# Neighbour choice kept as marks in the score tile, and turned into one-hots by TensorE and ScalarE

## The chip, the cores and the metric

The kernel runs on one core of one Trainium2 chip. The metric is the device time of one execution in microseconds (us); before the change the median of three runs is 13028.27 us, with 13025.54 and 13030.78 as the ends.

## The reference, cut to what matters

Two layers follow each other. Layer 0 cuts 16 images of 96 x 64 x 64 into windows of 8 x 8 pixels, finds for each of the 64 nodes of a window its nine nearest nodes, and takes the maximum of an edge function over them. Layer 1 is a state-space (Mamba) block, twice, over the 4096 pixels of each image, then a batch norm and a residual.

```python
nodes = win.reshape(Bw, C, WS * WS).transpose(0, 2, 1)      # Bw windows, 64 nodes, 96 channels
idx = knn_idx(nodes, K)                                      # K = 9 nearest by cosine distance, the node itself among them
x_j = jax.vmap(lambda n, i: n[i])(nodes, idx)
feat = jnp.concatenate([x_i, x_j - x_i], axis=-1)
h = jnp.einsum('bnkc,oc->bnko', feat, ew) + eb
h = jnp.max(gelu(h * es + et), axis=2)                       # over the nine neighbours
...
hstates = associative_scan(comb, (dA, dBx), axis=1)[1]       # layer 1, per image and layer
y = jnp.einsum('blds,bls->bld', hstates, Cm) + Dp * xc
```

## The kernel before

**Work and stages.** An image has eight rows of eight windows, 128 rows in all; a row has 512 pixels. Layer 0 works by rows, in two generators: `nearest` computes the scores of all node pairs and picks the eight nearest others, and `edges` gathers and evaluates them. Layer 1 works by items: 256 items, each one stretch of 512 pixels of one image in one of two layers, and an item has eight steps, one for each pair of states. These 2048 steps are the main loop.

**One step of the main loop.** `bcast` (L729, TensorE) spreads one row pair of the matrix B over the partitions into a PSUM tile `bt`, of which there is one buffer; `times_b` (L734, VectorE) multiplies it into `db` (PSUM, one buffer); the scan (L911, VectorE) runs over `da` and `db` into `hb`; GpSimd multiplies `hb` by C (L943); `folded` (L745, L747, TensorE) sums it into `y`. ScalarE makes `da` by three exponentials (L708), up to two steps ahead. `bt` of the next step is the first thing TensorE does in a step, `db` of the next step is made by VectorE after the scan, and `y` of the step before is folded last.

**What runs beside it.** The order on each engine is the order in which the program issues (`manual_schedule`). In each step the generators in `going` (an item's `norm`, `nearest`, `edges`, `tail`) are advanced by one `yield`, oldest first, and after them those in `preps` (`prelude`, the projections of the item after next). Products handed to `apart` are issued at the end of the step, and what uses them at the start of the next. From the ninth row on one row is started every 16 steps: `edges` of a row and `nearest` of the next one start in the same step, `nearest` ahead of `edges` in the list. Both have 16 stages of this kind, so a row takes 16 steps, and two items pass meanwhile. The first three rows run before the main loop (`drain`), and five rows after them run at twice the pace.

**The names used below.** The steps of one row's cycle are numbered 1 to 16. `edges` handles four of the eight windows in steps 1 to 8 and the other four in steps 9 to 16: three steps for the one-hot matrices `oh`, two for the products `pv` (L452, L453) and their copy `vu`, two for the gather products `t` (L468, L471) with their GELU (L476), one spare. In steps 8 and 16 `prelude` starts (`pj`, L608 and L620 with the Silu table), in steps 1 and 9 it goes on (`pj` L613, then the table of exp and ln again), in steps 2 and 10 come its product `pd` and the product `pow` of `tail` (L772), in steps 3 and 11 `pdta` (L646) with `e` and `rl` (L653, L654). In step 3 there are also `pf` of the next row's `nearest` (L340, its `y` at L343) and `pf2` of `edges` (L515). In step 4 `norm` issues `pc` (L581) with `sqv` (L583), and in step 5 `pvar` with `rs` (L588). In steps 6 and 14 the products with `dp_diag` (L742, L743) open a new `y`.

**PSUM.** `bt` takes one bank, `db` three, `y` two; all else shares the tag `mm` with two buffers. A new `mm` tile takes the buffer of the one before the last, and waits until that one has been read.

**The one-hots before.** VectorE's `max` gives the eight best scores of each node of a window pair, `max_index` their positions (L396, L909, in steps 12 to 15). The positions are written to DRAM (L401), read back onto 64 partitions by a broadcast DMA of 256 KB (L430), and compared with the partition's number: for one pair of windows by GpSimd (`is_equal`, L441), for the other by ScalarE (Abs L443, then Relu of 1 - x, L444).

Of the kernel before, what the change touches and what calls it, by code (L numbers as in the profile page):

```python
# [10 lines left out]
F32 = mybir.dt.float32  # L11
U16 = mybir.dt.uint16
BF16 = mybir.dt.bfloat16
AF = mybir.ActivationFunctionType
ALU = mybir.AluOpType
# [6 lines left out]
def tile_conv_knn_mamba(ctx: ExitStack, tc: tile.TileContext, w: dict, out: bass.AP):  # L22
# [8 lines left out]
    nc = tc.nc  # L31
# [4 lines left out]
    NN = WS * WS  # L36
    K = 9
    KO = K - 1
    NQ = H // WS
    NW = W // WS  # L40
    NP = NW // 2
    Q = 512
# [15 lines left out]
    const = ctx.enter_context(tc.tile_pool(name="const", bufs=1))  # L58
    dram1 = ctx.enter_context(tc.tile_pool(name="dram1", bufs=1, space=DRAM))
    dram = ctx.enter_context(tc.tile_pool(name="dram", bufs=3, space=DRAM))  # L60


    ident = const.tile([128, 128], F32, name="ident")
    make_identity(nc, ident)
    cmat = const.tile([C, C], F32, name="cmat")
    nc.vector.tensor_scalar(cmat, ident[:C, :C], -1.0 / C, None, ALU.add)
    node = const.tile([NN, 1], F32, name="node")
    nc.gpsimd.iota(node, pattern=[[0, 1]], base=0, channel_multiplier=1, allow_small_or_imprecise_dtypes=True)
    minus_node = const.tile([NN, 1], F32, name="minus_node")
    nc.vector.tensor_scalar(minus_node, node, -1.0, None, ALU.mult)  # L70
    neg1 = const.tile([128, 1], F32, name="neg1")
    nc.vector.memset(neg1, -1.0)
    eps_t = const.tile([128, 1], F32, name="eps_t")
# [4 lines left out]
    ohs = []  # L78
# [122 lines left out]
    pr = main.enter_context(tc.tile_pool(name="ring", bufs=2))  # L201
# [3 lines left out]
    pm = main.enter_context(tc.tile_pool(name="ps_m", bufs=2, space=PSUM))  # L205
# [102 lines left out]
    def half(h):  # L308
        return slice(h * CB, (h + 1) * CB)

    closing, opening, uses = [], [], []
# [17 lines left out]
    chosen_of = {}  # L329

    def nearest(b, q):

        nm = f"{b}_{q}"
        xr = pr.tile([C, Q], F32, tag="seq", name=f"x_{nm}", bufs=NSEQ)
        seqs[b, q] = xr
        nc.sync.dma_start(out=xr, in_=x[b].rearrange("c h w -> c (h w)")[:, bass.ts(q, Q)])
        yield
        yield
        pf = pm.tile([C, Q], F32, tag="mm", name=f"pf_{nm}")
        nc.tensor.matmul(pf, lhsT=fc1T, rhs=xr, start=True, stop=True)  # L340
        y = pr.tile([C, Q], F32, tag="y0", name=f"y_{nm}")
        nodes_of[b, q] = y
        nc.scalar.activation(  # L343
            y.rearrange("p (w r c) -> p r w c", w=NW, r=WS),
            pf.rearrange("p (r w c) -> p r w c", r=WS, w=NW),
            AF.Identity,
            bias=fc1_b[:, 0, :],
            scale=fc1_s[:, 0, :],
        )
        yield  # L350
        sq = pr.tile([C, Q], F32, tag="sq", name=f"sq_{nm}")
        nc.gpsimd.tensor_tensor(sq, y, y, ALU.mult)
        yield

        ss = pm.tile([C, Q], F32, tag="mm", name=f"ss_{nm}")
        nc.tensor.matmul(ss, lhsT=ones_cc, rhs=sq, start=True, stop=True)
        nc.scalar.copy(sq[0:1], ss[0:1])
        ss_d = dram.tile([1, Q], F32, tag="ss_d", name=f"ssd_{nm}")
        nc.sync.dma_start(out=ss_d, in_=sq[0:1])
        r4 = pr.tile([128, 2, QJ], F32, tag="r4", name=f"r4_{nm}")  # L360
        nc.sync.dma_start(out=r4[:, 1], in_=ss_d.rearrange("o (p j) -> (o p) j", j=QJ))
        yield
        yield

        nc.gpsimd.tensor_scalar(r4[:, 0], r4[:, 1], 1e-24, None, ALU.max)
        nc.gpsimd.tensor_tensor(r4[:, 0], r4[:, 0], mhalf, ALU.pow)
        nc.gpsimd.tensor_tensor(r4[:, 1], r4[:, 1], r4[:, 0], ALU.mult)
        nc.gpsimd.tensor_tensor(r4[:, 1], r4[:, 1], r4[:, 0], ALU.mult)
        yield
        r4_d = dram.tile([2, Q], F32, tag="r4_d", name=f"r4d_{nm}")  # L370
        nc.sync.dma_start(out=r4_d.rearrange("t (p j) -> p t j", j=QJ), in_=r4[:, 0:2])
        rn = pr.tile([C, Q], F32, tag="rs", name=f"rn_{nm}")
        nc.sync.dma_start(out=rn, in_=r4_d[0:1, :].to_broadcast([C, Q]))
        hs = hss[(b * NQ + q) % NHS]
        nc.sync.dma_start(out=hs[NN : NN + 1].rearrange("o w j -> o (w j)"), in_=r4_d[1:2, :])
        yield
        yield
        xn = pr.tile([C, Q], F32, tag="xn", name=f"xn_{nm}", bufs=1)
        nc.gpsimd.tensor_tensor(xn, y, rn, ALU.mult)
        yield  # L380


        sc = pm.tile([128, NP, NN], F32, tag="mm", name=f"sc_{nm}")
        hs4 = hs.rearrange("k (p h) j -> k p h j", h=2)
        for h in range(2):
            nc.tensor.matmul(sc[half(h)], lhsT=own, rhs=hs4[:, :, h, :], start=True, stop=False)
            for p in range(NP):
                nodes = xn[:, bass.ts(2 * p + h, NN)]
                nc.tensor.matmul(sc[half(h), p, :], lhsT=nodes, rhs=nodes, start=False, stop=(p == NP - 1))
        scs = pr.tile([128, NP, NN], F32, tag="scs", name=f"scs_{nm}", bufs=1)  # L390
        nc.scalar.copy(scs, sc)
        yield
        idx = pr.tile([128, NP, KO], U16, tag="idx", name=f"idx_{nm}")
        for p in range(NP):
            m1 = pr.tile([128, KO], F32, tag="m1", name=f"m1_{nm}_{p}")
            nc.vector.max(m1, scs[:, p, :])  # L396
            opening.append(partial(nc.vector.max_index, idx[:, p, :], m1, scs[:, p, :]))
            yield SLOT

        idx_d = dram.tile([NP, 128, KO], U16, tag="idx_d", name=f"idxd_{nm}")  # L400
        nc.sync.dma_start(out=idx_d.rearrange("p i k -> i p k"), in_=idx)  # L401
        chosen_of[b, q] = idx_d

    def taken():

# [10 lines left out]
    def edges(b, q):  # L416

        nm = f"{b}_{q}"
        y = nodes_of.pop((b, q))
        idx_d = chosen_of.pop((b, q))  # L420
        maxima = []

        def maximum(w):
# [2 lines left out]
                maxima.append(pr.tile([128, NP, NB3, NN], F32, tag="hq", name=f"hq_{nm}", bufs=1))  # L426
            return maxima[0][:, w]
        for hf in range(2):
            idb = pr.tile([NN, NP, NN * KO], U16, tag="idb", name=f"idb_{nm}_{hf}", bufs=1)
            nc.sync.dma_start(  # L430
                out=idb.rearrange("j w n -> j (w n)"),
                in_=idx_d.rearrange("(s p) i k -> s (p i k)", s=2)[hf : hf + 1].to_broadcast([NN, NP * NN * KO]),
            )
            yield


            for p in (1, 0):
                ohj = ohs[p][0:NN].rearrange("j w i k -> j w (i k)")
                numbers = idb[:, 2 * p : 2 * p + 2, :]
                if p == 0:  # L440
                    nc.gpsimd.tensor_scalar(ohj, numbers, node, None, ALU.is_equal)  # L441
                else:
                    nc.scalar.activation(ohj, numbers, AF.Abs, bias=minus_node)  # L443
                    nc.scalar.activation(ohj, ohj, AF.Relu, bias=1.0, scale=-1.0)  # L444
                yield
            vus = []
            for p in range(2):

# [11 lines left out]
            for p in range(2):  # L460
# [4 lines left out]
                for part in range(3):  # L465
# [9 lines left out]
                    j = part // 2  # L475
# [4 lines left out]
            if hf == 1:  # L480
# [8 lines left out]
                    bias=e_b[:, 0:1],  # L489
                    scale=e_s[:, 0:1],  # L490
# [3 lines left out]
                for h in range(2):  # L494
# [5 lines left out]
                    bias=e_b[:, 1:2],  # L500
                    scale=e_s[:, 1:2],
# [326 lines left out]

    FIRST = 3
    drain(nearest(0, 0))  # L830
    for q in range(FIRST):
        drain(nearest(0, q + 1), edges(0, q), *([prepared(q - 1)] if q else []))
    drain(nearest(0, FIRST + 1))

    AHEAD = 2
    order = [(n, p) for n in range(NI) for p in range(NPR)]
# [20 lines left out]
    bt = bcast(*order[0])  # L857
    db = times_b(*order[0], bt)
    going, preps = [several_at_once(edges(0, FIRST), 3)], []
    for _ in range(3):  # L860
        next(going[0])
# [3 lines left out]
    for r in range(FIRST + 1, NB * NQ):  # L865
        at = NPR * (r - FIRST) - 3 if r <= NQ else 16 * (r - NQ) + 29
        rows_at.setdefault(at, []).append((edges, r, 3 if r <= NQ else 1))
        if r > FIRST + 1:
            quick = r <= NQ + 1
            rows_at.setdefault(at - (9 if quick else 16), []).insert(0, (nearest, r, 2 if quick else 1))  # L870
    for m, (n, p) in enumerate(order):
        b, i, k = items[n]
        nm = f"{b}_{i}_{k}"
# [102 lines left out]
    with tc.tile_pool(name="bn", bufs=5) as pn:  # L976
        for b in range(NB):
            o = pn.tile([128, NJ, 1024], F32, tag="o", name=f"bo_{b}")
# [35 lines left out]
```

## Time and profile before

| | |
|---|---|
| median of three runs | 13028.27 us |
| the profiled execution | 13021.43 us |
| its span, first to last instruction | 13019.7 us |
| mean granted TensorE clock | 0.949 |
| VectorE busy | 11940.4 us (92%) |
| GpSimd busy | 11686.0 us (90%) |
| TensorE busy, matmuls | 11254.7 us (86%) |
| ScalarE busy | 10407.8 us (80%) |
| `oh` on GpSimd, L441 | 256 x 2855 ns |
| `oh` on ScalarE, L443 and L444 | 256 x 1134 ns and 256 x 1057 ns |
| first scan of the main loop | 263 us after the span's start |

The columns are times of one profiled execution on the one core. A line such as "L441 POOL TENSOR_SCALAR oh<-idb,node" is an instruction group by source line, engine and operation, with the tile it writes and those it reads. POOL is GpSimd, DVE VectorE, ACT ScalarE, PE TensorE, PEld its weight loads, SPq the queue on which the DMAs are issued. In a timeline a number in brackets is the idle time of that engine before the instruction, with what ended it.

### The profile page before, as it was taken

To read this page: it belongs to the slowest core of one execution; us is meant where nothing else is said; L and a number is where in the kernel's file an instruction comes from. 1 tells how busy PE (TensorE), PEld (TensorE's weight loads), DVE (VectorE), ACT (ScalarE), POOL (GpSimd) and SP (SyncE) were. 2 spreads that over 40 slices of the span, in tenths; PEclk is the share of its full clock that TensorE was granted. 3 is DMA by queue.
4 is the path that set the end of the run, shared out by engine and by line. 5 is a ranking of instruction groups with operands and counts; after the bars stand their busy time and mean duration, and the time that the engine had idled before them with its cause. 6 is when DMAs were issued, how large, how long until landed. Compare 5 with 4: busy or idle time off the path is not lost.

```text
span 13019.7 us, 155850 instructions
## 1 busy us (share of the span) xinstructions
PE 11254.7 (86%) x46920; PEld 4359.3 (33%) x46920; DVE 11940.4 (92%) x8270; ACT 10407.8 (80%) x16186; POOL 11686.0 (90%) x8644
## 2 busy tenths in 40 slices
PE   5889889888989989888888888988888888889872
PEld 2333333333333333333333333333333333333320
DVE  2699999999999999999999999999999999999995
ACT  4778888888888888888888888888888888888763
POOL 3699999999999999999999999999999999999993
PEclk8899999999999999999999999999999999999986
DMA  1233333333333333333333333333333333333336
GB/s 38 66 85 95 91 91 93 94 92 89 98 89 90 96 92 90 93 94 89 95 95 87 98 92 90 94 92 93 90 95 92 90 95 93 92 89 97 89 87 261
DMA packets 1031198, 1226.82 MB, mean 94 GB/s; under 512 B 429440, under 2 KB 560910, under 8 KB 1024208
## 3 DMA queue, kind: packets, MB, share of 16 engines
q1 hardware_dynamic: 1026352, 1191.59, 35.2%
q10 hardware_dynamic: 4000, 25.28, 0.5%
q8 instruction: 370, 6.06, 0.2%
q14 instruction: 476, 3.90, 0.1%
HBM read 706.83 MB, written 85.72 MB: 61 GB/s over the span
## 4 chain that ended last, share of the span: by engine, by line
POOL 27%; PE 19%; DVE 18%; ACT 13%; issue 9%; DMA 7%; SPq 6%; POOLq 0%; DVEq 0%; ACTq 0%
POOL hb L943 16%; DVE hb L911 11%; DVE db L734 6%; ACT da L708 5%; PE y L745 3%; SPq L690 2%; SPq L692 2%; DMA ct<-cd 2%; POOL ln L674 2%; PE t L468 2%; PE y L747 1%; PE pj L608 1%; PE t L471 1%; POOL hn L591 1%; POOL ln L676 1%
## 5 line engine op out<-in xcount | busy, mean ns | idle before, releaser
L943 POOL TENSOR_TENSOR hb<-hb,ct 128x1536 f32<-128x1536 f32 x2048 | 7091.9, 3463 | 313.5 <-DVE hb L911 78.4
L911 DVE TENSOR_TENSOR_SCAN hb<-da,db 128x1536 f32<-128x1536 f32 x2048 | 6863.5, 3351 | 216.6 <-ACT da L708 39.4
L708 ACT ACTIVATE da<-delta,a 128x511 f32<-128x511 f32 x6144 | 3937.7, 713 | 28.7 <-DVE hb L911 24.1
L734 DVE TENSOR_TENSOR db<-u,bt 128x1536 f32<-128x1536 f32 x2048 | 3605.3, 1760 | 386.6 <-PE bt L729 266.3
L745 PE MATMUL y<-hb,fold 128*64 128x512 f32 x8192 | 2273.8, 634 | 230.4 <-POOL hb L943 219.7
L476 ACT ACTIVATE da<-t,eb,es 128x512 f32<-128x512 f32 x1536 | 1181.3, 777 | 775.3 <-PE t L468 534.7
L747 PE MATMUL y<-hb,fold 128*64 128x256 f32 x8192 | 1259.5, 386 | 0.0
L729 PE MATMUL bt<-bparts,bsel 128*128 128x512 bf16 x2048 | 828.4, 404 | 462.4 <-DVE db L734 459.3
L468 PE MATMUL t<-oh,vu 128*128 128x512 f32 x2048 | 1012.8, 616 | 27.2 <-ACT da L476 14.1
L747 PEld LDWEIGHTS y<-hb,fold 128*64 128x64 f32 x8192 | 604.2, 141 | 1247.6 <-issue 1247.6
L413 DVE TENSOR_REDUCE hq<-da 128x192 f32<-128x1536 f32 x512 | 890.4, 1739 | 105.4 <-ACT da L476 105.4
L608 PE MATMUL pj<-hn,conv_in 128*128 128x512 f32 x2048 | 932.8, 598 | 0.9 <-POOL hn L591 0.9
L745 PEld LDWEIGHTS y<-hb,fold 128*64 128x64 f32 x8192 | 495.0, 141 | 1278.5 <-issue 528.6
L441 POOL TENSOR_SCALAR oh<-idb,node 64x1024 f32<-64x1024 uint16 x256 | 731.0, 2855 | 117.2 <-DMA idb<-idxd 111.6
L452 PE MATMUL pv<-ewT,y 96*64 96x192 f32 x2048 | 477.6, 360 | 335.2 <-ACT rs L588 253.4
L942 POOL COPY state<-hb 128x3 f32<-128x3 f32 x1792 | 397.5, 222 | 392.3 <-DVE hb L911 359.0
L620 ACT ACTIVATE xc<-pj,conv_b 128x512 f32<-128x512 f32 (+1 forms) x512 | 297.2, 580 | 510.5 <-PE pj L613 397.8
L471 PE MATMUL t<-oh,vu 128*64 128x512 f32 x2048 | 560.4, 626 | 167.0 <-ACT da L476 162.3
L608 PEld LDWEIGHTS pj<-hn,conv_in 128*128 128x128 f32 x2048 | 396.4, 194 | 386.5 <-issue 375.7
L613 PE MATMUL pj<-hn,conv_in 128*64 128x256 f32 x4096 | 514.4, 394 | 0.0
L452 PEld LDWEIGHTS pv<-ewT,y 96*64 96x64 f32 x2048 | 253.0, 143 | 774.4 <-ACT rs L588 358.4
L468 PEld LDWEIGHTS t<-oh,vu 128*128 128x128 f32 x2048 | 373.5, 194 | 402.9 <-issue 290.3
(180 smaller groups left out, 17972.0 us busy)
## 6 DMA issues: line engine op xcount, KB each, us to landing
ct<-cd SPq DMA_DIRECT2D x4096, 128.0 KB
delta<-ln SPq DMA_DIRECT2D x1024, 128.0 KB
u<-s SPq DMA_DIRECT2D x1024, 128.0 KB
idb<-idxd SPq DMA_DIRECT2D x256, 256.0 KB
delta<-ln SPq DMA_DIRECT2D x1024, 64.0 KB
u<-s SPq DMA_DIRECT2D x1024, 64.0 KB
x<-in_x SPq DMA_DIRECT2D x128, 192.0 KB
rn<-r4d SPq DMA_DIRECT2D x128, 192.0 KB
```

The costliest lines, as they stand in the source:

```text
L413: nc.vector.tensor_reduce(out(), g.rearrange("p s (i k) -> p s i k", k=KO), AX.X, ALU.max)
L441: nc.gpsimd.tensor_scalar(ohj, numbers, node, None, ALU.is_equal)
L468: nc.tensor.matmul(t, lhsT=vus[p][:, part, :128], rhs=ohw[part], start=True, stop=True)
L476: nc.scalar.activation(g, t, AF.Gelu, bias=e_b[:, j : j + 1], scale=e_s[:, j : j + 1])
L608: nc.tensor.matmul(ps, lhsT=wt[:, t, :128], rhs=hn[:, off : off + Q], start=(t == 0), stop=(t == taps - 1))
L708: nc.scalar.activation(da[:, c, 1:Q], delta[:, c, 1:], AF.Exp, scale=a_neg[i][:, c, p : p + 1])
L729: nc.tensor.matmul(bt, lhsT=bsel[:, p, :], rhs=made[n][2], start=True, stop=True)
L734: nc.vector.tensor_tensor(db, made[n][5], bt.unsqueeze(1).to_broadcast([128, NB3, Q]), ALU.mult)
L745: nc.tensor.matmul(y[half(h), 0], lhsT=fold, rhs=hb[:, h, :], start=False, stop=(p == NPR - 1))
L747: nc.tensor.matmul(y[half(h), 1, :QH], lhsT=fold, rhs=hb[:, 2, bass.ts(h, QH)], start=False, stop=(p == NPR - 1))
L911: nc.vector.tensor_tensor_scan(*(t.rearrange("p c q -> p (c q)") for t in (hb, das[at], db)), 0.0, ALU.mult, ALU.add)
L943: nc.gpsimd.tensor_tensor(hb, hb, ct.unsqueeze(1).to_broadcast([128, NB3, Q]), ALU.mult)
```

## The change

The positions are not computed any more. `match_replace` (VectorE) overwrites the eight best scores in the score tile by a mark, 2^20. Eight small products with the identity turn the marked tile, so that the neighbours lie on partitions, into an `mm` tile, and ScalarE makes 0/1 marks `mt` (bfloat16) of it. For each window pair two bfloat16 products in one `mm` tile add up, for each node i, place k and candidate j, the number of marks that precede j, plus 100 if j itself is marked, minus 100, minus k: zero exactly where j is the k-th marked neighbour of i. ScalarE takes Abs (`off`, bfloat16) and then, by two instructions, Relu of 1 - x into the one-hot tile. GpSimd has no part in it, and both DMAs are gone. The stages stay as many as before.

```diff
-    node = const.tile([NN, 1], F32, name="node")
-    nc.gpsimd.iota(node, ...)
-    minus_node = ...
+    FAR = 100.0
+    MARK = 2.0**20
+    before = const.tile([128, 128], BF16, name="before")
+    sel0 = const.tile([128, 128], BF16, name="sel0")
+    krow = const.tile([128, Q], BF16, name="krow")
...
@@ nearest
-        idx = pr.tile([128, NP, KO], U16, tag="idx", name=f"idx_{nm}")
         for p in range(NP):
             m1 = pr.tile([128, KO], F32, tag="m1", name=f"m1_{nm}_{p}")
             nc.vector.max(m1, scs[:, p, :])
-            opening.append(partial(nc.vector.max_index, idx[:, p, :], m1, scs[:, p, :]))
+            opening.append(partial(nc.vector.match_replace, scs[:, p, :], m1, scs[:, p, :], MARK))
             yield SLOT
-        idx_d = dram.tile([NP, 128, KO], U16, tag="idx_d", name=f"idxd_{nm}")
-        nc.sync.dma_start(out=idx_d.rearrange("p i k -> i p k"), in_=idx)
-        chosen_of[b, q] = idx_d
+        ps = pm.tile([128, NP, NN], F32, tag="mm", name=f"mp_{nm}")
+        for h in range(2):
+            for p in range(NP):
+                nc.tensor.matmul(
+                    ps[half(h), p, :], lhsT=scs[half(h), p, :], rhs=ident[half(h), half(h)], start=True, stop=True
+                )
+        mt = pr.tile([128, NP, NN], BF16, tag="mt", name=f"mt_{nm}", bufs=3)
+        nc.scalar.activation(mt, ps, AF.Relu, bias=neg1, scale=2.0 / MARK)
+        chosen_of[b, q] = mt
@@ edges
         for hf in range(2):
-            idb = pr.tile([NN, NP, NN * KO], U16, tag="idb", name=f"idb_{nm}_{hf}", bufs=1)
-            nc.sync.dma_start(out=idb..., in_=idx_d....to_broadcast([NN, NP * NN * KO]))
-            yield
-            for p in (1, 0):
-                ohj = ohs[p][0:NN].rearrange("j w i k -> j w (i k)")
-                numbers = idb[:, 2 * p : 2 * p + 2, :]
-                if p == 0:
-                    nc.gpsimd.tensor_scalar(ohj, numbers, node, None, ALU.is_equal)
-                else:
-                    nc.scalar.activation(ohj, numbers, AF.Abs, bias=minus_node)
-                    nc.scalar.activation(ohj, ohj, AF.Relu, bias=1.0, scale=-1.0)
-                yield
+            def ranks(p):
+                ps = pm.tile([128, NN, KO], F32, tag="mm", name=f"rk_{nm}_{hf}_{p}")
+                nc.tensor.matmul(ps, lhsT=sel0, rhs=krow.rearrange("o (i k) -> o i k", k=KO), start=True, stop=False)
+                marks = mt[:, 2 * hf + p, :].unsqueeze(2).to_broadcast([128, NN, KO])
+                nc.tensor.matmul(ps, lhsT=before, rhs=marks, start=False, stop=True)
+                off = pr.tile([128, NN, KO], BF16, tag="off", name=f"off_{nm}_{hf}_{p}")
+                nc.scalar.activation(off, ps, AF.Abs)
+                return off
+            def onehot(p, off):
+                for h in range(2):
+                    nc.scalar.activation(ohs[p][0:NN, h], off[half(h)], AF.Relu, bias=1.0, scale=-1.0)
+            off = ranks(1)
+            yield
+            onehot(1, off)
+            off = ranks(0)
+            yield
+            onehot(0, off)
+            yield
```

More of the change, by code (lines that the diff above doesn't have):

```diff
@@ L66, in tile_conv_knn_mamba @@
     nc.vector.tensor_scalar(cmat, ident[:C, :C], -1.0 / C, None, ALU.add)
-    node = const.tile([NN, 1], F32, name="node")
-    nc.gpsimd.iota(node, pattern=[[0, 1]], base=0, channel_multiplier=1, allow_small_or_imprecise_dtypes=True)
-    minus_node = const.tile([NN, 1], F32, name="minus_node")
-    nc.vector.tensor_scalar(minus_node, node, -1.0, None, ALU.mult)
+    FAR = 100.0
[3 more added lines that the diff above has]
+    krow = const.tile([128, Q], BF16, name="krow")
+    nc.vector.memset(sel0, 0.0)
+    nc.vector.memset(sel0[0:1], 1.0)
+    nc.vector.memset(krow, 0.0)
+    for k in range(KO):
+        nc.vector.memset(krow[0:1].rearrange("o (i k) -> o i k", k=KO)[:, :, k], -FAR - k)
+    with tc.tile_pool(name="order", bufs=1) as sp:
+        lower = sp.tile([128, 128], F32, name="lower")
+        nc.gpsimd.memset(lower, 1.0)
+        nc.gpsimd.affine_select(
+            out=lower, in_=lower, compare_op=ALU.is_gt, fill=0.0, base=0, pattern=[[1, 128]], channel_multiplier=-1
+        )
+        nc.vector.memset(lower[:NN, NN:], 0.0)
+        nc.vector.scalar_tensor_tensor(before, ident, FAR, lower, ALU.mult, ALU.add)
     neg1 = const.tile([128, 1], F32, name="neg1")
@@ L396, in nearest @@
             nc.vector.max(m1, scs[:, p, :])
-            opening.append(partial(nc.vector.max_index, idx[:, p, :], m1, scs[:, p, :]))
+            opening.append(partial(nc.vector.match_replace, scs[:, p, :], m1, scs[:, p, :], MARK))
             yield SLOT
-        idx_d = dram.tile([NP, 128, KO], U16, tag="idx_d", name=f"idxd_{nm}")
-        nc.sync.dma_start(out=idx_d.rearrange("p i k -> i p k"), in_=idx)
-        chosen_of[b, q] = idx_d
+        ps = pm.tile([128, NP, NN], F32, tag="mm", name=f"mp_{nm}")
[3 more added lines that the diff above has]
+                    ps[half(h), p, :], lhsT=scs[half(h), p, :], rhs=ident[half(h), half(h)], start=True, stop=True
+                )
+        mt = pr.tile([128, NP, NN], BF16, tag="mt", name=f"mt_{nm}", bufs=3)
+        nc.scalar.activation(mt, ps, AF.Relu, bias=neg1, scale=2.0 / MARK)
+        chosen_of[b, q] = mt
     def taken():
@@ L419, in edges @@
         y = nodes_of.pop((b, q))
-        idx_d = chosen_of.pop((b, q))
+        mt = chosen_of.pop((b, q))
         maxima = []
@@ L428, in edges @@
         for hf in range(2):
-            idb = pr.tile([NN, NP, NN * KO], U16, tag="idb", name=f"idb_{nm}_{hf}", bufs=1)
[L430 to L433, printed above, removed]
-            yield
-            for p in (1, 0):
-                ohj = ohs[p][0:NN].rearrange("j w i k -> j w (i k)")
-                numbers = idb[:, 2 * p : 2 * p + 2, :]
-                if p == 0:
-                    nc.gpsimd.tensor_scalar(ohj, numbers, node, None, ALU.is_equal)
-                else:
-                    nc.scalar.activation(ohj, numbers, AF.Abs, bias=minus_node)
-                    nc.scalar.activation(ohj, ohj, AF.Relu, bias=1.0, scale=-1.0)
-                yield
+            def ranks(p):
[10 more added lines that the diff above has]
+            off = ranks(1)
+            yield
+            onehot(1, off)
[3 more added lines that the diff above has]
+            yield
             vus = []
```

## The prediction

> **What bounds the kernel now.** I read the page first.
>
> ```profile
> PE 11254.7 (86%) x46920; PEld 4359.3 (33%) x46920; DVE 11940.4 (92%) x8270; ACT 10407.8 (80%) x16186; POOL 11686.0 (90%) x8644
> ```
>
> Four engines are at 80 to 92%, so the shares don't say which one a saving would move. I took the scan starts (L911) out of VectorE's timeline. The loop's first 45 steps take 426.5 us, 9.5 each; after them scans 64 to 1904 take 97.26 us for each cycle of 16 steps. The shortest form of each step in those cycles sums to 95.2 us, in which VectorE never waits. So VectorE is the bound and stands still for 2.0 us a cycle. The waits from 1200 to 12000 us say for whom:
>
> ```profile
> DVE db L734 <- PE bt L729: 162.9, 141, 3.0
> DVE hb L911 <- PE y L747: 26.4, 35, 2.4
> DVE db L907 <- POOL first L723: 8.1, 19, 1.1
> ```
>
> It waits for TensorE and hardly ever for GpSimd, although GpSimd is 90% busy. Next the timeline of VectorE, a step with a neighbour search and one without:
>
> ```profile
> 6022.64 3.35 DVE L911 TENSOR_TENSOR_SCAN hb<-da,db 128x1536 f32<-128x1536 f32 x1
> ...
> 6028.03 0.22 DVE L909 FIND_INDEX8 idx<-m,scs 128x8 uint16<-128x64 f32 x1
> 6028.19 3.35 DVE L911 TENSOR_TENSOR_SCAN hb<-da,db 128x1536 f32<-128x1536 f32 x1
> ...
> 6070.79 3.35 DVE L911 TENSOR_TENSOR_SCAN hb<-da,db 128x1536 f32<-128x1536 f32 x1
> ...
> 6076.35 3.35 DVE L911 TENSOR_TENSOR_SCAN hb<-da,db 128x1536 f32<-128x1536 f32 x1
> ```
>
> 5.55 us with the search, 5.56 without: the search lies in gaps. Then the timeline of TensorE from step 3 to step 7 (in this cycle step 1 scans at 6047.92, 2 at 6053.47, 3 at 6059.68, 4 at 6065.26, 7 at 6081.90), with `pf2` and the `bt` of steps 4, 6 and 7:
>
> ```profile
> 6063.31 1.10 PE L515 MATMUL pf<-x,ident 96*96 96x512 f32 x2 [0.59 <-ACT rl L654]
> ...
> 6067.51 0.39 PE L729 MATMUL bt<-bparts,bsel 128*128 128x512 bf16 x1
> ...
> 6075.70 0.38 PE L452 MATMUL pv<-ewT,y 96*64 96x192 f32 x1 [2.06 <-ACT rs L588]
> ...
> 6076.50 0.61 PE L729 MATMUL bt<-bparts,bsel 128*128 128x512 bf16 x1
> ...
> 6085.45 0.39 PE L729 MATMUL bt<-bparts,bsel 128*128 128x512 bf16 x1
> ```
>
> and ScalarE beside it:
>
> ```profile
> 6055.74 1.14 ACT L443 ACTIVATE oh<-idb,minus_node 64x1024 f32<-64x1024 uint16 x1
> ...
> 6060.92 0.77 ACT L343 ACTIVATE y<-pf,fc_b,fc_s 96x512 f32<-96x512 f32 x1
> 6062.17 0.60 ACT L653 ACTIVATE e<-pdta 128x512 f32<-128x512 f32 x1 [0.47 <-PE pdta L646]
> ```
>
> From step 15 to step 7 TensorE is one chain: over all cycles it idles 0.0 us in step 16, 0.0 in 1, 0.14 in 2 and 0.65 in 3 (for `rl`); in steps 4 and 5 its idle time (0.7 and 2.1) waits for ScalarE's `sqv` and `rs`, which themselves wait for TensorE's `pc`. Its `bt` of step 4 is done 0.85 us before VectorE takes it (mean), that of step 7 only 0.04 us, after a stall of 1.0. So what is added to TensorE or ScalarE in steps 16 to 3 comes out in step 7 in full. In the other half TensorE has 1.2 us idle in step 12 and 3.1 in step 14, where `bt` waits for `db`: a lag ends there.
>
> **Part by part, per cycle (119 of them).**
>
> *GpSimd* loses 2 x 2.855 us (L441). VectorE waits for GpSimd by itself 8.1 us in 112 cycles; the 26.4 us for `y` hang on late `hb` too. TensorE waits 1.1 us for `hb` in step 8, but the next `bt` has 3.1 us to spare there. Gain 0 to 0.35; I take 0.3. The scan takes 3341, 3353 and 3356 ns (least, median, most) beside whatever GpSimd runs, so nothing more comes from there. [...]
>
> *VectorE*: `max_index` (80 + 218 ns) becomes `match_replace`, which no row shows; the nearest, MAX8 over the same 64 elements, takes 202. Four a cycle in the same gaps: 0, as for the search now; uncovered 4 x 0.3 = 1.2 us, below zero nothing, since the pair costs nothing today.
>
> *SP's queue* loses three DMAs a cycle; `ct`, `delta` and `u` behind them go out 0.5 us sooner, and nothing on VectorE's side waits for them: 0. Where they are exposed, in the first 690 us, the chain of waits carries idxd, idb and the one-hots with about 78 us (4.7, 2 and 6.5% of the first 263 us, 4.9, 2.6 and 2.8% of the next 427). There the new products and activations follow one another, for eight rows about 8 x (1.3 + 2 x 2.3) = 47 us. Net -30, from -78 to +20.
>
> *Step 16*: eight products of 64 columns, 16 instructions on TensorE. The last eight of L389 take 0.56 us to the next start (6013.18 to 6013.74), so 1.0 (0.6 to 1.2). The marks' Relu on ScalarE, 0.39 (L653's form of 256), delays `xc` to about 6049.9.
>
> *Step 1*: two bfloat16 products, each 0.22 us to the next start after `bt`: 0.45 (0.4 to 0.9, if the operand repeated eight times streams at half the rate). `pj` L613 behind them needs the buffer that `xc` frees: 0.1. TensorE is now 1.55 late, ScalarE too after `z`; Abs (0.60, L653) fits into its waits of 0.95 and 0.63 for `pj`.
>
> *Step 2*: two products, 0.45, then `pd`; `pow` is now the second `mm` tile after the ranks and needs their Abs read. That Abs sits on ScalarE behind `z` (late, to 6054.1), the table load (1.28), `da` (1.94) and two Relus of 64x512 (1.1 together; L444 took 1057 ns for the same elements, L654 592 for 512): it ends at 6059.05. `pow`, at 6055.44 now, could start at 6057.4 and waits 1.6. TensorE is 3.6 late.
>
> *Step 3*: two more Relus, 1.1, lie between `y` (L343) and `e`; ScalarE's idle 0.47 no longer covers them, since `y` waits for a late `pf`. `e` and `rl` come 0.85 later than `pdta` would let them, and `pf2` waits for `rl`.
>
> Sum: 1.0 + 0.55 + 0.45 + 1.6 + 0.85 = 4.45 us on the chain. VectorE stalls before the `db` that end steps 3 and 4, for about 3.6, and for the rest at the end of step 7. With products at the low end and no wait, 1.5; with the repeated operand slow and the clock low after the new waits (after the wait of 2.06 the next `bt` took 0.61 instead of 0.39), 5.8. `da` isn't late: in steps 2 to 6 it is done 2 to 6 us before its scan.
>
> *Steps 9 to 11*: the same without the turn; TensorE some 1.2 late, ScalarE 1.9, given back in steps 12 to 14: 0.1 (0 to 0.4).
>
> Per cycle 4.45 + 0.1 - 0.3, about 4.2; 119 x 4.2 = 500; with -30, +470. The profiled execution took 13021.4 us for a span of 13019.7, 6.8 below the median of 13028.3. So 13491 by the profile, 13498 by the median.
>
> Abs in steps 1 and 9 stands between two Silu activations; no row shows Abs under that table, only under that of exp and ln. If it needed another table, two loads of 1283 ns would come into step 1's chain: 2.6 us a cycle more. [...]
>
> **The rivals.** *TensorE's own time alone* (18%): the `mm` buffers are free in time and ScalarE's Relus fit into its 16 us of idle a cycle. For it: ScalarE is only 83% busy. Against: order, not load, places them. 1.9 x 119 - 30 = +196: 13224, from 13100 to 13350.
>
> *Relief wins* (12%): GpSimd's queue, up to 6.4 us behind the scan in step 7, and `y` behind it hold TensorE more than the waits tell; without `oh` the chain into step 7 starts earlier. It decides if TensorE reaches `bt` of step 4 less than 0.85 us later than now. Half of the 2.0 us of stalls goes, and 50 us at the start: -170, 12858; with all of both, -316.
>
> *Both cancel* (4%): within 0.2%, 26 us, which is about what a measurement of this kernel can tell from no change.
>
> *The Silu table lacks Abs* (4%): +305 more, 13800.
>
> **How the numbers follow.** The chain of waits has 62%, and its 4.45 (3 to 5.8) gives 13340 to 13720. The range from 13000 to 13720 takes in it, TensorE's own time and no change; left out are relief, the table and the tails, 20%. Faster 0.12, the same 0.04, slower 0.84.
>
> **What would show it.** Right: the cycle at 101 us; VectorE's waits for `bt` near 600 us, most of them in steps 3 and 4; TensorE's `pow` waiting for ScalarE's `off` in step 2 and `pf2` for `rl` over 1 us; `match_replace` steps at 5.55; GpSimd at 83 to 86%, waiting for VectorE; the loop's first scan earlier. Wrong: `pow` starting without a wait, or steps 3 and 4 at 5.55 us.

## The result, and the profile after

| | before | after |
|---|---|---|
| median of five runs | 13030.78 us | 13740.98 us (13727.81 to 13756.10) |
| span of the profiled execution | 13019.7 us | 13739.2 us |
| first scan of the main loop | 263.3 us | 247.9 us |
| the loop's first 45 steps | 426.5 us | 412.7 us |
| cycle of 16 steps, scans 64 to 1904 | 97.26 us | 103.61 us |
| what follows the last scan's start | 206.1 us | 206.1 us |

The ratio is 1.0545 (95% interval 1.0531 to 1.0559): slower by 5.5%, 21 us beyond the top of the predicted range. The part ahead of the steady cycle became 29 us shorter, and each cycle 6.35 us longer (119 x 6.35 = 756; with the 29 off that is 727, where the span grew by 719.5).

The page's line of busy times, to be held against that of before:

```profile
PE 11638.1 (85%) x49992; PEld 4553.0 (33%) x49992; DVE 11952.4 (87%) x8282; ACT 10817.6 (79%) x17338; POOL 10990.9 (80%) x8389
```

Every share fell or stayed: no engine became the bound by its load. VectorE does as much as before (11952 against 11940 us) in a longer span. GpSimd has 695 us less to do and the kernel got nothing for it. The waits from 1200 to 12600 us (sum, number, longest):

```profile
DVE db L759 <- PE bt L754: 772.3, 440, 4.6
POOL state L967 <- DVE hb L936: 767.5, 617, 4.5
POOL e L697 <- ACT s L687: 686.3, 219, 6.4
...
PE pow L797 <- ACT off L456: 322.6, 220, 1.8
...
PE pf L540 <- ACT rl L679: 162.8, 111, 1.5
```

The first line was 165.7 us over the same stretch before. Its growth, 607 us, is most of the loss (110 cycles of 6.35 us are 698): VectorE stands still for `bt`, which TensorE brings late. The last two say what TensorE waits for: Abs (`off`) in steps 2 and 10 and `rl` in step 3, both ScalarE's. The timelines show it in one cycle, first TensorE from step 1 to step 3:

```profile
6050.73 0.38 PE L452 MATMUL rk<-krow,sel 128*128 128x512 bf16 x1
6050.95 0.38 PE L454 MATMUL rk<-mt,before 128*128 128x512 bf16 x1
...
6054.76 1.10 PE L797 MATMUL pow<-z,out_w 128*96 128x512 f32 x2 [1.59 <-ACT off L456]
...
6063.19 1.10 PE L540 MATMUL pf<-x,ident 96*96 96x512 f32 x2 [1.47 <-ACT rl L679]
```

then ScalarE beside it,

```profile
6052.97 1.25 ACT L462 ACTIVATE oh<-off 64x512 f32<-64x512 bf16 x2
6054.13 0.57 ACT L456 ACTIVATE off<-rk 128x512 bf16<-128x512 f32 x1
...
6060.92 1.26 ACT L462 ACTIVATE oh<-off 64x512 f32<-64x512 bf16 x2
6062.08 0.57 ACT L678 ACTIVATE e<-pdta 128x512 f32<-128x512 f32 x1
```

and VectorE, where it comes out:

```profile
6061.52 3.35 DVE L936 TENSOR_TENSOR_SCAN hb<-da,db 128x1536 f32<-128x1536 f32 x1
6067.81 1.76 DVE L759 TENSOR_TENSOR db<-u,bt 128x1536 f32<-128x1536 f32 x1 [2.94 <-PE bt L754]
...
6069.88 3.35 DVE L936 TENSOR_TENSOR_SCAN hb<-da,db 128x1536 f32<-128x1536 f32 x1
```

Two Relus stand ahead of `off`, and two more ahead of `e`. `pow` waits for the first pair, `pf2` for the second, and step 4 takes 8.36 us from scan to scan. `pow` waits 1.59 where 1.6 was forecast. `pf2` waits 0.88 longer than before's 0.59, where 0.85 was forecast.

Where the 6.35 us lie (mean duration of the steps over the 115 cycles from scan 64 to 1904; the steps left out differ by less than 0.06):

| step | 3 | 4 | 5 | 6 | 7 | 13 | 14 | 15 |
|---|---|---|---|---|---|---|---|---|
| before | 5.55 | 5.49 | 5.51 | 5.96 | 7.92 | 5.55 | 5.82 | 6.13 |
| after | 6.29 | 8.49 | 5.62 | 6.42 | 8.24 | 6.30 | 5.87 | 7.10 |

Steps 3 to 7 grew by 4.6 us, steps 13 to 15 by 1.76. The first number was forecast, the second was not.

### The profile page after: what moved, and what is told of

It reads as the page before. It is cut to its first block, busy times and chain, and to the rows that moved or that the text cites. A ratio compares the mean times of both kernels' runs of the same rounds, so it can differ in the third digit from the quotient of the medians.

```text
span 13739.2 us, 162638 instructions
## 1 busy us (share of the span) xinstructions
PE 11638.1 (85%) x49992; PEld 4553.0 (33%) x49992; DVE 11952.4 (87%) x8282; ACT 10817.6 (79%) x17338; POOL 10990.9 (80%) x8389
## 4 chain that ended last, share of the span: by engine, by line
PE 42%; ACT 36%; POOL 8%; issue 6%; DVE 3%; DMA 3%; SPq 2%; ACTq 0%; POOLq 0%; DVEq 0%
ACT da L733 13%; PE y L770 6%; PE pj L633 5%; POOL hb L968 5%; PE t L493 4%; PE t L496 4%; PE pj L638 3%; PE y L772 3%; ACT oh L462 3%; PE bt L754 2%; ACT L652 2%; PE pow L797 2%; DVE hb L936 2%; ACT da L501 2%; PE pow L799 1%
## 5 line engine op out<-in xcount | busy, mean ns | idle before, releaser
L936 DVE TENSOR_TENSOR_SCAN hb<-da,db 128x1536 f32<-128x1536 f32 x2048 | 6863.6, 3351 | 296.3 <-PE y L772 71.4
L697 POOL TENSOR_TENSOR e<-e,s 128x768 f32<-128x768 f32 x256 | 464.9, 1816 | 756.2 <-ACT s L687 755.2
L493 PE MATMUL t<-oh,vu 128*128 128x512 f32 x2048 | 1005.6, 613 | 14.8 <-ACT da L501 14.5
L462 ACT ACTIVATE oh<-off 64x512 f32<-64x512 bf16 x1024 | 638.2, 623 | 6.9
L797 PE MATMUL pow<-z,out_w 128*96 128x512 f32 x512 | 282.8, 634 | 348.2 <-ACT off L456 347.4
```

What stands on the lines that cost most here:

```text
L462: nc.scalar.activation(ohs[p][0:NN, h], off[half(h)], AF.Relu, bias=1.0, scale=-1.0)
L493: nc.tensor.matmul(t, lhsT=vus[p][:, part, :128], rhs=ohw[part], start=True, stop=True)
L936: nc.vector.tensor_tensor_scan(*(t.rearrange("p c q -> p (c q)") for t in (hb, das[at], db)), 0.0, ALU.mult, ALU.add)
```

## The experiments

The theory is that of the prediction, called order: the time goes where an instruction is put ahead of one that TensorE waits for. The rival is load: TensorE or ScalarE have more to do, wherever it stands. The runs were made in four series, in which the kernel before took 13018.80 to 13032.28 us; each ratio is taken within its own series, and a difference of times between two series is good to some 12 us.

**The second Abs ahead of the first Relus.** In steps 2 and 10 the products and Abs of p = 0 are issued before the Relus of p = 1; nothing else moves.

```diff
-            onehot(1, off)
-            off = ranks(0)
+            off1, off = off, ranks(0)
+            onehot(1, off1)
             yield
```

> The changed kernel with one edit: in step 2 the products and the Abs of the second ranks are issued before the two Relus of the first. The load of every engine stays the same. Theory of order (the loss comes from ScalarE work that TensorE waits for through the two mm buffers): pow's wait for off, 1.6 us in step 2 and about 1.45 in step 10, shrinks by the 1.16 us of the two Relus; about 1.2 us less per cycle in the half with steps 16 to 7 and up to 0.8 in the other; 240 us less than the changed kernel, near 13500. Rival of load (TensorE's and ScalarE's added busy time sets it): no change, 13740. Rival that the lag is made in step 3 by the Relus in front of e and rl: half the gain, since ScalarE then waits for pf as before, 13620.

Measured: 13490.63 us (13486.24 to 13502.37), ratio 1.0355 (1.0338 to 1.0373). The same instructions on the same engines, 250 us less. TensorE's wait of `pow` for `off` fell from 322.6 to 57.7 us.

**The Relus of p = 0 one step sooner**, behind their Abs in steps 2 and 10 instead of ahead of `e` and `rl` in 3 and 11.

```diff
             onehot(1, off)
             off = ranks(0)
-            yield
             onehot(0, off)
             yield
+            yield
```

> The changed kernel with one edit: the second pair of Relus is issued in step 2, right behind its Abs, instead of in step 3 in front of e and rl. Same load. Theory of order: pf2's wait for rl, 1.47 us, falls to about 0.3; e, s and sqv come 1.2 us earlier in step 11 and 12, where ScalarE stood still 2.9 us for the scores; 1.2 us less per cycle in one half, about 1.0 in the other: 260 us less than the changed kernel, near 13480; pow's wait for off stays. Rival of load: 13740.

Measured: 13513.16 us (13511.18 to 13513.88), ratio 1.0372 (1.0355 to 1.0389): 228 us less, and `pf2` waits 59.5 us for `rl` instead of 162.8.

**Both.**

```diff
-            onehot(1, off)
-            off = ranks(0)
-            yield
+            off1, off = off, ranks(0)
+            onehot(1, off1)
             onehot(0, off)
             yield
+            yield
```

> Both edits: second Abs first, then all four Relus in step 2. Same load. Theory of order: the two terms add up; the half with steps 16 to 7 keeps the products' own 1.9 us and little else, the other half loses nearly all of its 1.7 us: 3.6 us less per cycle, near 13310. Rival of load: 13740. If the two edits hit the same wait: about 13480, as the better of the two alone.

Measured: 13355.46 us (13352.43 to 13365.52), ratio 1.0253 (1.0235 to 1.0270). Order alone is worth 385 us of the 710 (382 with each kernel held against its own series). The two gains add up to 478 when taken singly, so they overlap; the time lies between the 13310 of terms that add up and the 13480 of a common wait. VectorE's and TensorE's waits in this run:

```profile
DVE db L759 <- PE bt L754: 507.2, 321, 3.0
...
PE pf L540 <- ACT rl L679: 68.4, 113, 0.7
...
PE pow L797 <- ACT off L456: 58.4, 142, 0.7
```

**The products alone.** The kernel before, one-hots by its own way, with the new products added on constants where the changed kernel has them, and read by nobody.

```diff
+        ps = pm.tile([128, NP, NN], F32, tag="mm", ...)        # step 16
+        ... eight products of 64 columns
...
+            ranks(1)                                           # steps 1, 9
...
+                    ranks(0)                                   # steps 2, 10
```

> The kernel before with TensorE's new products added at their places in steps 16, 1, 2, 9 and 10 (8 small ones, and 4 pairs of bfloat16 products on constant operands), read by nobody; positions, DMAs and one-hots as before. Theory of order: the products cost their own time on the chain, 1.2 to 1.9 us per cycle, some of it swallowed by the 0.65 us wait for rl in step 3: 13170 to 13250. Rival of load with TensorE as the cause: most of the loss is here, 13500 or more. Rival that ScalarE alone makes it: 13030 to 13060.

Measured: 13227.08 us (13224.45 to 13237.64), ratio 1.0155 (1.0138 to 1.0172). The cycle is 1.75 us longer, most of it in steps 4 (+1.0) and 7 (+0.55). *TensorE's own time alone* had been priced at 1.9 a cycle, and that price holds; it is one term of the loss, not the loss. That the time lies so near the rival's 13224 is chance: the rival's sum has 30 us off for the part ahead of the loop, which this run leaves nearly as it was.

**ScalarE alone.** The kernel before with both window pairs' one-hots by ScalarE and no product added.

```diff
-                if p == 0:
-                    nc.gpsimd.tensor_scalar(ohj, numbers, node, None, ALU.is_equal)
-                else:
-                    nc.scalar.activation(ohj, numbers, AF.Abs, bias=minus_node)
-                    nc.scalar.activation(ohj, ohj, AF.Relu, bias=1.0, scale=-1.0)
+                nc.scalar.activation(ohj, numbers, AF.Abs, bias=minus_node)
+                nc.scalar.activation(ohj, ohj, AF.Relu, bias=1.0, scale=-1.0)
```

> The kernel before with one edit: the one-hots that GpSimd built by comparison are built by ScalarE (Abs, then Relu), from the turned positions, so no product is added and TensorE does what it did; ScalarE does as many steps as in the changed kernel. Theory of order (what is put ahead of e and r_l in steps 3 and 11 goes into the cycle): two more pairs of instructions, 583 + 623 ns each, are issued per half, 1.2 to 2.4 us of them ahead of e and r_l in each half; 119 x 2.5 to 4 = 300 to 480 us: about 13400. Rival (the changed kernel lost its time to TensorE's added products alone, ScalarE's share of 79% being far from full): 13000 to 13080.

Measured: 13492.64 us (13491.85 to 13508.92), ratio 1.0351 (1.0335 to 1.0367). The cycle is 3.9 us longer, 1.08 of it in steps 13 and 15. The time is within what was expected, but the load is another one than the expectation says: the edit issues one more pair per half, of 1138 and 1057 ns. ScalarE so gets 4.4 us more per cycle, where the changed kernel gives it 3.4, and 2.2 us stand ahead of `e` and `rl`, there 1.25. The granted clock was 0.933 to 0.935 in these runs and 0.945 to 0.948 before. So ScalarE's steps cost hundreds of us at these places with no product added, but the 460 us are not the part that they have in the 710.

**GpSimd's relief alone.**

```diff
+        nc.vector.memset(oh[0:NN], 0.0)
...
-                    nc.gpsimd.tensor_scalar(ohj, numbers, node, None, ALU.is_equal)
+                    pass
```

> The kernel before with GpSimd's comparisons left out: the one-hots of the second half of each pair are not built (their buffers are zeros, written once), so that half of the gathered rows are zero; TensorE and ScalarE do all that they did. It shows what relieving GpSimd alone is worth. Theory of order (GpSimd's work lies off the chain in all but a few places): 0 to 0.35 us per cycle, 0 to 42 us, and some 17 us ahead of the loop: 12960 to 13028, about 13000. Rival (GpSimd binds a good part of the cycle): 12850 or less.

Measured: 13017.76 us (13011.58 to 13028.35), ratio 0.9987 (0.9977 to 0.9996). Its cycle takes 97.4 us, before's 97.3: nothing was gained in the loop, as far as a trace can tell (the last run below, which does in the loop what the kernel before does, has 97.4 too). What was gained lies ahead of it, 7.7 us to the first scan and 3.5 in the next 45 steps. The mean scan is as long as with GpSimd's comparisons (3351 ns before):

```profile
L912 DVE TENSOR_TENSOR_SCAN hb<-da,db 128x1536 f32<-128x1536 f32 x2048 | 6864.1, 3352 | 231.8 <-ACT da L709 50.1
```

**As many products, elsewhere.** The kernel before with some 1.8 us of products a cycle, all in steps 9 and 10, where the prediction saw room on TensorE.

```diff
+            def ranks(p):
+                for twice in range(2 * hf):                    # steps 9 and 10 only, each pair twice
+                    rank(p, twice)
```

> The kernel before with as much added product time on TensorE per cycle as in the run that had the products alone (some 1.8 us), all of it in steps 9 and 10, none in steps 16 to 2; nothing reads the results. Theory of order: steps 9 and 10 hold TensorE time that no one waits for, 0 to 0.2 us per cycle, 13030 to 13050. Rival (a busy TensorE costs what it is given wherever it stands): as in the run with the products alone, about 13230.

Measured: 13162.64 us (13152.75 to 13164.15), ratio 1.0099 (1.0083 to 1.0114). Neither number: 130 us where order gave 0 to 20 and load 200. The cycle is 1.15 us longer, 0.22 of it in step 13 and 0.76 in step 15. The expectation has the two runs equal in product time, which they are not: the run with the products alone had 2.8 us, only two of these four pairs in steps 9 and 10 (0.9 us) and its other 1.9 us in steps 16 to 2; its steps 13 and 15 grew by 0.1 together. So by these two runs the room there is near 0.9 us, an estimate, and what exceeds it comes out in the steps that the prediction had called safe. Place matters, as order says, but steps 9 and 10 are no free place.

**The order of steps 9 to 11 alone.** The changed kernel, with both edits of order in the second half of the cycle only. It asks where the unforeseen 1.76 us come from.

```diff
-            onehot(1, off)
+            off1 = off
+            if hf == 0:
+                onehot(1, off1)
             off = ranks(0)
+            if hf == 1:
+                onehot(1, off1)
+                onehot(0, off)
             yield
-            onehot(0, off)
+            if hf == 0:
+                onehot(0, off)
             yield
```

> The changed kernel with one edit in steps 9 to 11 alone: the rank products and Abs of the pair p = 0 are issued ahead of the other pair's Relus, and its own Relus in step 10 instead of step 11, where they stood ahead of e and r_l. Steps 1 to 3 stay as in the changed kernel. Theory of order (steps 13 and 15 are 1.65 us longer than forecast because of these Relus): steps 13 and 15 shrink by 1.0 to 1.5 us as they did in the run that had the new order in both halves, 119 x 1.25 = 150 us: 13590, from 13540 to 13640. Rival (steps 13 and 15 are long because steps 1 to 7 hand on their delay): no change, 13720 to 13750.

Measured: 13571.81 us (13559.07 to 13575.06), ratio 1.0421 (1.0403 to 1.0438): 169 us less (157 with each kernel held against its own series). Step 13 went from 6.30 to 5.59 us and step 15 from 7.10 to 6.40, together 1.4, and 119 x 1.4 = 167; steps 3 to 7 stayed (35.0 us in sum in both kernels). The whole cycle is 1.55 us shorter, some 184 us, of which the loop's first 45 steps, 11.5 us longer here, give a little back. The rival, a delay handed on from steps 1 to 7, falls.

How it works is read from one cycle of each kernel. `sqv`, which the product `po` waits for (it is there in 58 of the 115 cycles), comes behind `e` and `s` on ScalarE. TensorE, before the change, in step 12:

```profile
4848.54 1.10 PE L787 MATMUL po<-x,fusT 96*96 96x512 f32 x2 [1.78 <-ACT sqv L583]
4849.57 1.08 PE L745 MATMUL y<-hb,fold 128*64 128x512 f32 x4
...
4851.01 0.39 PE L729 MATMUL bt<-bparts,bsel 128*128 128x512 bf16 x1
```

ScalarE after the change, from step 11:

```profile
6007.44 0.38 ACT L405 COPY scs<-sc 128x256 f32<-128x256 f32 x1 [2.94 <-PE sc L403]
6007.70 1.27 ACT L462 ACTIVATE oh<-off 64x512 f32<-64x512 bf16 x2
6008.88 0.57 ACT L678 ACTIVATE e<-pdta 128x512 f32<-128x512 f32 x1
...
6013.95 0.57 ACT L608 ACTIVATE sqv<-pc 96x512 f32<-96x512 f32 x1
```

and TensorE and VectorE behind it:

```profile
6014.58 1.86 PE L812 MATMUL po<-x,fusT 96*96 96x512 f32 x2 [2.27 <-ACT sqv L608]
6016.36 1.97 PE L770 MATMUL y<-hb,fold 128*64 128x512 f32 x4
...
6018.69 0.39 PE L754 MATMUL bt<-bparts,bsel 128*128 128x512 bf16 x1
```
```profile
6019.12 1.76 DVE L759 TENSOR_TENSOR db<-u,bt 128x1536 f32<-128x1536 f32 x1 [1.61 <-PE bt L754]
```

With the new order in that half, the wait is back at its length, and so are the products:

```profile
5949.91 1.10 PE L818 MATMUL po<-x,fusT 96*96 96x512 f32 x2 [1.77 <-ACT sqv L614]
5950.94 1.08 PE L776 MATMUL y<-hb,fold 128*64 128x512 f32 x4
```

The clock that TensorE was granted in the changed kernel, ahead of that wait and behind it (columns: stretch, its length, TensorE's busy time, granted clock, DMA share, GB/s):

```profile
6010.00:6012.30 2.30, 2.30 (x15) 1.00 0.05 7
6014.50:6018.20 3.70, 3.62 (x8) 0.54 0.37 112
```

So in this cycle the late `sqv` costs twice: the wait itself, and products at about half the clock behind it, 1.65 us more for `po` and the `y` after it. In the 58 cycles with `po`, the mean start of `sqv` after the scan of step 12 went from 3.25 to 5.58 us (+2.33), the end of the next `bt` from 7.54 to 10.34. VectorE asks for it at 9.00, so 1.46 us were to spare before and 1.34 are missing after. Step 13 is 1.47 us longer in these cycles (5.55 before), and not at all in the others. The wait is the larger share: in the 29 cycles in which `po` kept its length step 13 takes 6.63 us, in the 29 in which it was slow 7.41. In step 15 it is the GELU that comes late; the next lines of the same cycle:

```profile
6028.80 1.98 PE L496 MATMUL t<-oh,vu 128*64 128x512 f32 x4 [2.47 <-ACT da L501]
...
6033.02 1.76 DVE L759 TENSOR_TENSOR db<-u,bt 128x1536 f32<-128x1536 f32 x1 [2.27 <-PE bt L754]
```

Over the 115 cycles the wait of `t` in step 15 went from 0.95 to 1.66 us.

**Half of the Relus to GpSimd**, on top of the new order in both halves.

```diff
-                for h in range(2):
-                    nc.scalar.activation(ohs[p][0:NN, h], off[half(h)], AF.Relu, bias=1.0, scale=-1.0)
+                nc.gpsimd.tensor_scalar(ohs[p][0:NN, 0], off[half(0)], 0.0, None, ALU.is_equal)
+                nc.scalar.activation(ohs[p][0:NN, 1], off[half(1)], AF.Relu, bias=1.0, scale=-1.0)
```

> The kernel with the new order in both halves, and two of the four Relus of each half given to GpSimd as comparisons of the turned ranks with 0; ScalarE has 1.25 us less to do per half. Theory of order: what is left over the kernel before at 13355 is part products (13227 with them alone) and part ScalarE's steps; half of the latter goes: 13250 to 13340, about 13290. Rival (all that is left comes from the products and the wait for Abs): 13350 to 13370. Rival (GpSimd's comparisons come later than ScalarE's Relus and the gathers wait for them): above 13370.

Measured: 13314.48 us (13307.36 to 13317.41), ratio 1.0224 (1.0207 to 1.0241): 41 us below the run without it (33 with each held against its own series), within what was expected. With order mended, this much less on ScalarE is a small part of what is left; the products (200 us) are the larger one. GpSimd's two comparisons of 1492 ns per half may hide a part of the gain.

**Marks ahead of the loop, positions in it.** The saving and the loss lie in different places, so both ways can be had.

```diff
+    LAST = 8
+    def marked(b, q):
+        return b * NQ + q <= LAST
...
+            if marked(b, q):
+                ...  # match_replace, mp and mt, ranks, Abs, Relus as in the changed kernel
+            else:
+                ...  # positions, idx_d, idb and is_equal as before
...
-        b3 = pr.tile([128, 3, QS], BF16, tag="b3", name=f"b3_{nm}")
+        b3 = pr.tile([128, 3, QS], BF16, tag="b3", name=f"b3_{nm}", bufs=1)
```

> A hybrid: the changed kernel's path (marks, turned by TensorE, rank products, ScalarE's one-hots) for the rows up to 8, which lie ahead of the steady loop, and the kernel before's path for all others. The trace of after has its first scan 15.4 us sooner and its first 45 steps 13.8 us shorter than before. Theory of order (the change saves ahead of the loop and loses in the loop's cycle alone): 13027 - 29 = about 13000, from 12990 to 13020. Rival (the saving ahead of the loop is given back when the cycle settles): 13020 to 13040.

Measured: 12998.86 us (12997.13 to 13011.11) against 13032.28, ratio 0.9975 (0.9964 to 0.9985): 33 us, or 0.25%, below the kernel before where 29 were expected; small, but the interval does not reach 1. Its first scan comes at 246.9 us, its next 45 steps take 411.1, and its cycle 97.4, before's 97.3. What `b3` with one buffer does by itself was not run.

## Why the prediction was wrong in its size

The direction was right, and so were the mechanism and its price in steps 16 to 7; the sum was some 250 us short (470 forecast for the span, 719.5 measured), and one term, steps 9 to 11, holds most of it. The top of the range, 13720, is 13028 and 119 x 5.8: it leaves no room for that term, not even for its own 0.4.

- *Step 16*, *Step 1*, *Step 2*, *Step 3*: 4.45 forecast, 4.6 measured in steps 3 to 7 (119 x 0.15, some 18 us). The parts fit too: 16 small products 0.89 to 0.96 us against 1.0, a pair of rank products 0.45 against 0.45, the waits as shown above. VectorE's stalls ahead of the `db` that end steps 3 and 4 are 3.9 us, 3.7 more than before, against 3.6. The rest was forecast for the end of step 7; 0.3 came there, 0.6 in steps 5 and 6.
- *Steps 9 to 11* is the step that failed: "given back in steps 12 to 14: 0.1 (0 to 0.4)". It measured 1.76, 119 x 1.66 = 198 us more. It had the lags nearly right (TensorE 1.2 and ScalarE 1.9 late; `sqv` was 2.33 late), but set them against "1.2 us idle in step 12". That idle time was itself TensorE's wait for ScalarE's `sqv`: it is room for a late TensorE, none for a late ScalarE. Counted as a chain from `sqv` to `bt`, the room in cycles with `po` is 1.46 us, less than the 2.33. The 3.1 us in step 14 are behind that point, and the GELU has its own chain into step 15. The run with steps 9 to 11 reordered took back 1.4 of the 1.76.
- *GpSimd*: 0.3 a cycle taken, 0 found in the run without its comparisons; 36 us.
- *SP's queue* and the part ahead of the loop: -30 forecast, -29 measured. The balance came; its two parts, 78 saved and 47 added, were not measured apart.
- *VectorE*: `match_replace` takes 208 ns and its load of values 81, where 202 and 80 were taken from neighbours; step 12, which holds it, lasts 5.53 us (5.55 before). The growth of steps 13 and 15 isn't its doing: the run with steps 9 to 11 reordered keeps `match_replace`, and its step 13 is back at 5.59 us; the run of ScalarE alone searches by `max_index`, and its steps 13 and 15 are 1.08 us longer all the same.

18 + 198 + 36 + 1 is 253, against a shortfall of 249.5; 119 full cycles are a round figure in the forecast and here. Of the signs named ahead, `pow` waiting for `off`, `pf2` for `rl` and the earlier first scan came as said; of the steps with `match_replace`, step 12 stayed at its length, steps 13 and 15 did not. The cycle is 103.6 instead of 101 us, VectorE's waits for `bt` 772 instead of 600 us, GpSimd 80% instead of 83 to 86%.

*The Silu table lacks Abs* did not happen. ScalarE's timeline in step 1:

```profile
6043.59 1.28 ACT L645 ACT_TABLE_LOAD   x1
6044.89 0.69 ACT L645 ACTIVATE xc<-pj,conv_b 128x512 f32<-128x512 f32 x1
6045.80 0.60 ACT L456 ACTIVATE off<-rk 128x512 bf16<-128x512 f32 x1 [0.23 <-PE rk L454]
6047.69 0.47 ACT L645 ACTIVATE xc<-pj,conv_b 128x256 f32<-128x256 f32 x1 [1.29 <-PE pj L638]
```

Abs runs between two Silus (0.69 and 0.47 us) with no load between them, and the trace has 1050 table loads after the change as before. That the forecast's sum counts no load for Abs was the author's assumption; no trace of the kernel before showed it. *Relief wins* and *TensorE's own time alone* were each tried by themselves and gave -14.5 and +200 us.

What stays open: of the 710 us the new order takes back 385 with the same instructions, and the products by themselves cost 200. The remaining 130 or so are not placed; half of the Relus taken off ScalarE were worth 33 to 41 of them. The wait of `pow` for the buffer that Abs holds (322.6 us in the changed kernel, none in the kernel before) exists only when products and Abs come together; a third `mm` buffer, which by the author's estimate would take it away by itself, was not tried.

## What to carry to other kernels

Idle time on an engine is room only for a delay that arrives through that engine: before setting a lag against it, read what ended the idle time, and if it was a wait for the engine that becomes late, follow that chain to the bound and take the room at its end. Work moved from an idle-looking engine to another is priced by the instruction it is put ahead of; here the same instructions in another order were worth 385 us, and GpSimd's 695 us of freed time nothing in the loop. Average a step over the cycles in which the waiting instruction is there, not over all of them.

## What the runs showed of the hardware

- TensorE's products were slow more often behind longer waits. In the cycle shown the granted clock was 0.54 behind a wait of 2.27 us. Over the 58 cycles with `po`, this product took over 1.3 us instead of 1.10 in 29 of them with the wait at 2.27 us (the changed kernel), in 34 of them with the same wait in the run with the second Abs first, and in 33 with 2.56 us (ScalarE alone). With 1.77 to 1.78 us, as in the nine other kernels, it was 7 to 21 of 58: 17 before the change, 12 with the second half reordered. The mean clock of the span was 0.949 before and after the change and doesn't show this. Nor does the length of the wait by itself sort the cycles: in the changed kernel it is 2.26 to 2.27 us ahead of the 29 slow `po` and of the 29 others alike. What lowers the clock behind such a wait is not shown.
- GpSimd's `e` (L697) waited for ScalarE's `s` for 686 us after the change and 1.4 before. It cost next to nothing: over the same stretch (1200 to 12600 us) VectorE waited 21.5 us in all for that `e`, and TensorE's own waits for `hb` fell from 187 to 18 us.
